# Moving three small VectorE operations ahead of two additions, and turning round the first score products of one visit in six

## The chip, the cores and the metric

The kernel runs on one core of a Trainium2 chip. The metric is the device time of one execution in microseconds (us). The engines are named as in the profile: PE is TensorE's matmul side, PEld its weight loads, DVE is VectorE, ACT is ScalarE, POOL is GpSimd, SP is SyncE.

## The reference

The input is x, 32 images of 256 channels and 32 x 32 positions, all in float32. For each image:

```python
h = _gn(x)                                  # group norm: 32 groups of 8 channels
q, k, v = 1x1 convolutions of h             # 8 heads of 32 channels, 1024 tokens
scores = q k^T / sqrt(32), kept only where key < query
out = x + softmax(scores) v
```

The group norm takes the mean and the variance of each group of eight channels over all positions. The mask is strict: a token doesn't see itself, and the first token's attention is zero.

## The kernel before

**Staging.** The kernel works through the images in one long pipeline of visits. An image has two channel groups `g` of 128 channels (four heads each), and a group has six visits (`VISITS`, L557), so an image has `N` = 12 visits. A visit computes scores of some key blocks against some query ranges for all four heads, exponentiates them on ACT, and adds the results up for the softmax's denominators on DVE. Keys lie on the partitions, so the exponentials go straight into the second product as the moving operand.

**The loop around the change** is at L705. In iteration i it calls, in this order:

1. `scores(i)` (L339): products into three two-bank PSUM tiles `sT` (L302), then three exponentials on ACT, into `e` (L384) and `eh` (L380), and, where the visit touches the diagonal, two masks on POOL (`mask`, L330).
2. what is listed in `at` for i: projections of a coming image (`pp` and `ppv`, L162) and some steps of older images.
3. `values(i - 1)` (L399): products of the exponentials of the visit before with v, into `acc` (L409).
4. `add_keys(i - 1)` (L421): the additions on DVE (L427), one to three of them.
5. what is listed in `after` for i: preparation of a coming image, output of an older one (`finish`, L521: `num` and `rb` on DVE, then a store), sums of denominators through DMAs.

[...] `FINISH` (L627) puts outputs of the image two before at the visits 1, 2 and 4, and `finish` of one visit precedes the preparation of the next.

**Preparation of an image** is `prepare` (L611) with the offsets `PREPARE` (L624), counted in visits from the image's first. It has ten steps: statistics of the two channel groups (`norm_channels`, L172), `norm_mean` (L180: four small products of `mv` with the averaging matrix into `pm`, and its eviction on ACT to `mean`), `norm_deviation` (L188: three DVE operations on 128 x 2 elements, L195 to L197, which wait for `mean`), `norm_variance` (L200: the second statistics product `pv`, which waits for `dev`, and its eviction to `rstd`), `norm_rstd` (L211, on POOL), and four times `norm_apply` (L221, on ACT). `norm_mean` and `norm_deviation` both stand at offset -9, `norm_variance` at -8, all of them in `after`. PSUM tiles for `pm`, `pv`, and half of the projections come from one pool with a single buffer (`misc`, L124), so `pv` also waits until the projection before it has been copied out (`v`, L266). Image 0's preparation runs ahead of the loop, image 1's has a list of offsets of its own (L668), and images 2 to 31 use `PREPARE` (L678).

**Scores of a visit.** The heads 0 to 3 of a group take 32 rows of the array each, and the two halves of a 128-key block take 64 columns each, so there are eight tiles of 32 x 64. A float32 product is carried out in two passes, which have a record each in the trace. An entry of a visit's list is "long" (to the `sT` tiles of heads 0, 1 and of heads 2, 3) or "short" (to the third tile). A `pair` (L282) is a short entry made of two products for each half: one 128 columns wide and one 64 wide, on the diagonal. `scores_of` (L307) carries out an entry's products by their place n in the pair: all 128-column ones first, then, after a call of `between`, the 64-column ones. `scores` does first the shorts of heads 2 and 3, then the longs of heads 0 and 1 (from the last entry of the list to the first), then the first long of heads 2 and 3, and then, behind a semaphore, the shorts of heads 0 and 1, and what is left.

Visit 0 of each group has two longs, of 384 and of 128 columns, and a pair; it is at `PAIRS` (L566). Visit 5 has two longs of the same widths and a short of 256 columns, and is not in `PAIRS`. The other four have a single long of 512 columns.

## Time and profile before

| | |
|---|---|
| median of 3 runs | 1832.91 us (1831.83 to 1835.73) |
| the profiled execution's own time | 1833.38 us |
| its span, first to last instruction | 1831.7 us |
| granted TensorE clock | 0.998 |
| DVE, busy share of the span | 91% |
| ACT, busy share of the span | 79% |
| DMA queues, share of 16 engines | 36.4% (software), 27.1% (hardware) |
| time of a whole image in the middle of the run | 56.1 us |

The page gives the busy time of each engine, then the chain of work that ended last, then groups of instructions with what ended the idle time before them. A line of the timeline begins with the start in us from the span's start and the duration; `x16` is the number of records merged in it, and the bracket at its end is the idle time of the engine before it and who ended it. The records of matmuls are pipelined: their starts are measured and their ends are modelled, so that a record can start ahead of the end of the one before.

### The profile page before, as it was taken

Reading aid. Unit: us, or ns where it says so; the run is one execution under the profiler, and the core shown is the slowest. Engines: PE = TensorE matmul, PEld = TensorE weight load, DVE = VectorE, ACT = ScalarE, POOL = GpSimd, SP = SyncE. Lnnn points to the kernel's source line nnn. Section 1 sums busy time; section 2 is a strip of 40 time slices with the busy share of each in tenths; the row PEclk is TensorE's granted clock in tenths of the full one; section 3 lists DMA queues with packets and bytes.
Section 4 is the critical chain, followed back from the end, with each engine's and each line's share of the span. In section 5 each row is a group of like instructions: output and inputs, shape, how many; then the busy total and the mean of one; then the engine's idle time right before and its main releaser. Section 6 shows DMA issues by size and latency. Waiting matters only on the chain.

```text
span 1831.7 us, 81670 instructions
## 1 busy us (share of the span) xinstructions
PE 1798.4 (98%) x37036; PEld 961.7 (53%) x37036; DVE 1667.8 (91%) x1831; ACT 1454.9 (79%) x1985; POOL 780.6 (43%) x901
## 2 busy tenths in 40 slices
PE   9999999999999999999999999999999999999997
PEld 5555555555555555555555555555555555555553
DVE  4689999999999999999999999999999999899988
ACT  6888878888778888788887788877888878788784
POOL 2344444444443444444434444444444344343431
PEclk9999999999999999999999999999999999999999
DMA  3457676676766676666767666667667676666652
GB/s 122 72 97 145 129 141 118 133 150 128 141 124 134 135 144 128 139 122 133 148 129 146 117 133 145 132 133 137 128 130 143 129 140 119 133 144 132 124 112 84
DMA packets 86531, 236.77 MB, mean 129 GB/s; under 512 B 21281, under 2 KB 22305, under 8 KB 70305
## 3 DMA queue, kind: packets, MB, share of 16 engines
q0 software_dynamic: 15872, 97.53, 36.4%
q1 hardware_dynamic: 70304, 133.96, 27.1%
q8 instruction: 290, 4.75, 1.1%
q14 instruction: 65, 0.52, 0.1%
HBM read 66.85 MB, written 34.57 MB: 55 GB/s over the span
## 4 chain that ended last, share of the span: by engine, by line
PE 93%; DVE 6%; issue 1%; ACT 0%; POOL 0%; DVEq 0%; POOLq 0%
PE sT L302 30%; PE pp L162 26%; PE acc L409 25%; PE ppv L162 10%; DVE e L427 3%; DVE dev L196 1%; DVE dev L197 1%; PE pd L461 1%; PE pv L162 0%; PE busy L148 0%; DVE rb L533 0%; ACT e L384 0%; DVE diagonal L427 0%; DVE dev L195 0%; PE pm L162 0%
## 5 line engine op out<-in xcount | busy, mean ns | idle before, releaser
L384 ACT ACTIVATE e<-sT 128x1024 f32<-128x1024 f32 x768 | 744.5, 1022 | 256.5 <-PE sT L302 232.2
L330 POOL TENSOR_SCALAR_AFFINE_SELECT diagonal<-eh 128x512 f32<-128x512 f32 x512 | 515.2, 1028 | 892.0 <-ACT eh L380 892.0
L302 PE MATMUL sT<-q,k 32*64 32x128 f32 (+2 forms) x18432 | 584.8, 372 | 3.3 <-issue 3.1
L427 DVE TENSOR_TENSOR e<-e,e 128x1024 f32<-128x1024 f32 x314 | 549.7, 1751 | 25.7 <-ACT v L266 6.3
L302 PEld LDWEIGHTS sT<-q,k 32*64 32x64 f32 x18432 | 406.1, 131 | 183.4 <-PE sT L302 59.4
L162 PE MATMUL pp<-xn,wT 128*32 128x512 f32 x4096 | 494.2, 598 | 0.9 <-issue 0.7
L409 PE MATMUL acc<-e,v 128*32 128x512 f32 (+3 forms) x4608 | 403.5, 450 | 0.0
L380 ACT ACTIVATE eh<-sT 128x768 f32<-128x768 f32 (+1 forms) x384 | 341.7, 890 | 0.0
L409 PEld LDWEIGHTS acc<-e,v 128*32 128x32 f32 x4608 | 150.1, 110 | 260.8 <-issue 238.3
L162 PE MATMUL ppv<-wT,xn 128*32 128x256 f32 x4096 | 248.5, 382 | 0.0
L162 PEld LDWEIGHTS pp<-xn,wT 128*32 128x32 f32 x4096 | 107.5, 109 | 201.4 <-issue 166.4
L427 DVE TENSOR_TENSOR diagonal<-diagonal,e 128x1536 f32<-128x1536 f32 x126 | 188.3, 1495 | 17.0 <-PE acc L409 9.2
L427 DVE TENSOR_TENSOR e<-e,eh 128x1024 f32<-128x1024 f32 x126 | 181.5, 1441 | 6.8 <-ACT xn L235 0.5
L427 DVE TENSOR_TENSOR e<-e,diagonal 128x2048 f32<-128x2048 f32 x63 | 144.0, 2286 | 36.8 <-POOL diagonal L330 36.8
L409 PEld LDWEIGHTS acc<-diagonal,v 128*32 128x32 f32 x4096 | 123.1, 110 | 86.8 <-issue 75.3
L162 PEld LDWEIGHTS ppv<-wT,xn 128*32 128x32 f32 x4096 | 120.9, 109 | 79.9 <-issue 7.8
L409 PE MATMUL acc<-diagonal,v 128*32 128x128 f32 x4096 | 161.2, 273 | 0.0
L440 POOL DMA_DIRECT2D diagonal<-diagonal x124 | 111.5, 899 | 64.3 <-DMA diagonal<-diagonal 64.3
L235 ACT ACTIVATE xn<-x,shift,rstd 128x256 f32<-128x256 f32 x248 | 137.1, 613 | 0.0
L528 DVE SCALAR_TENSOR_TENSOR rb<-num,v_bias_col,x 128x256 f32<-128x256 f32 x248 | 117.7, 515 | 4.4
L440 POOL DMA_DIRECT2D e<-e x124 | 102.2, 824 | 38.2 <-issue 38.2
L526 DVE TENSOR_TENSOR num<-num,rb 128x512 f32<-128x512 f32 x124 | 110.7, 893 | 0.5 <-DMA rb<-inverses 0.5
(78 smaller groups left out, 1026.1 us busy)
## 6 DMA issues: line engine op xcount, KB each, us to landing
diagonal<-diagonal POOLq DMA_DIRECT2D x62, 512.0 KB, 6.4
e<-e POOLq DMA_DIRECT2D x62, 512.0 KB, 5.6
rb<-inverses SPq DMA_DIRECT2D x124, 256.0 KB, 4.6
out_dram<-rb SPq DMA_DIRECT2D x124, 256.0 KB, 5.2
x<-in_x_dram SPq DMA_DIRECT2D x120, 256.0 KB, 5.8
diagonal<-diagonal POOLq DMA_DIRECT2D x62, 256.0 KB, 4.9
folded<-diagonal SPq DMA_DIRECT2D x62, 256.0 KB, 3.3
e<-e POOLq DMA_DIRECT2D x62, 256.0 KB, 5.1
```

The source lines that it names most:

```text
L162: nc.tensor.matmul(out[part], lhsT=lhsT[:, part], rhs=rhs, start=start, stop=stop, skip_group_check=True)
L196: nc.vector.tensor_mul(dev, dev, dev)
L235: nc.scalar.activation(to, of, AF.Identity, bias=live["shift", b][:, g : g + 1], scale=rstd)
L302: return nc.tensor.matmul(bank[c : c + KEYS, cols], lhsT=live["k", b, g][rows, kb * P + c : kb * P + c + KEYS], rhs=live["q", b, g][rows, ...
L330: nc.gpsimd.affine_select(out=square[:, :, place + s * P : place + (s + 1) * P], in_=raw[:, :, (1 - s) * KEYS : (3 - s) * KEYS], pattern=[ ...
L380: exp = nc.scalar.activation(eh.rearrange("p (n bank) q -> p bank n q", n=2)[:, :, :, :narrow], short[:, :, :, :narrow], AF.Exp)
L384: nc.scalar.activation(e[:, 2 * a : 2 * a + 2, :wide], pairs[a][:, :, :wide], AF.Exp)
L409: nc.tensor.matmul(acc[HD * j : HD * (j + 1), of], lhsT=live["v", b][:, kb, h * HD : (h + 1) * HD], rhs=e[:, j, :], start=first, stop=last ...
L427: nc.vector.tensor_add(to, to, tile_of(b, g, at))
L440: nc.gpsimd.dma_start(out=total[:rows], in_=total[rows : 2 * rows], accum_op=ALU.add)
L526: nc.vector.tensor_mul(num, num, rb)
L528: nc.vector.scalar_tensor_tensor(blocks(rb, s), blocks(num, s, s == 1), v_bias_col[:, g : g + 1], blocks(xt[:, g, cols], s), ALU.add, ALU.add,
```

## The change

Two things are changed.

- A third list, `between`, is carried out between `values` and `add_keys` of an iteration. For the images 2 to 31, `prepare` puts `norm_mean` and `norm_deviation` there (the steps with k = 2 and 3), in the same iteration as before.
- `scores_of` takes an order for the places n. In visits that have two longs and a pair, which is visit 0 of each group, the shorts of heads 2 and 3 begin with the 64-column products; the 128-column long of heads 0 and 1 follows as their `between`, then come the 128-column products of the pair, and then the 384-column longs. The shorts of heads 0 and 1 keep their order.

```diff
-        def scores_of(b, g, bank_of, heads, entries, between=lambda: None):
+        def scores_of(b, g, bank_of, heads, entries, between=lambda: None, order=slice(None)):
...
-                for n in range(max(map(len, halves))):
-                    if n:
+                for k, n in enumerate(list(range(max(map(len, halves))))[order]):
+                    if k:
                         between()
...
-            first = short_of((2, 3))
-            for n in range(len(longs) - 1, -1, -1):
-                long_of((0, 1), n)
+            begin = [lambda n=n: long_of((0, 1), n) for n in range(len(longs) - 1, -1, -1)]
+            if i in PAIRS and len(longs) > 1:
+                first = short_of((2, 3), begin.pop(0), slice(None, None, -1))
+            else:
+                first = short_of((2, 3))
+            for f in begin:
+                f()
             long_of((2, 3), 0)
...
-        at, after = {}, {}
+        at, between, after = {}, {}, {}
...
                 if n is None:
                     f()
+                elif isinstance(n, tuple):
+                    when(n[0], f, between)
                 else:
                     when(n, f, after)
...
-                    prepare(b, [first + n for n in PREPARE])
+                    prepare(b, [(first + n,) if k in (2, 3) else first + n for k, n in enumerate(PREPARE)])
...
                     values(b, v)
+                    for f in between.pop(i, ()):
+                        f()
                     if b < B - 1 or v not in SUMMED or v == 1:
                         add_keys(b, v)
```

More of the change, by code (lines that the diff above doesn't have):

```diff
@@ L348, in scores @@
             short = pairs[2].rearrange("p bank (n q) -> p bank n q", n=2)
-            short_of = lambda heads, *between: scores_of(
-                b, g, lambda j: short[:, j % 2, j // 2, :], heads, shorts, *between
+            short_of = lambda heads, *how: scores_of(
+                b, g, lambda j: short[:, j % 2, j // 2, :], heads, shorts, *how
             )
@@ L722, in unshifted @@
                     f()
-            assert not at and not after
+            assert not at and not between and not after
             outside = end_last(B - 1)
```

## The prediction

> **What bounds the kernel now.** I read the page's first part, then the list of waits, then the timeline at the two places that the diff touches. First the busy time of the engines:

> ```profile
> PE 1798.4 (98%) x37036; PEld 961.7 (53%) x37036; DVE 1667.8 (91%) x1831; ACT 1454.9 (79%) x1985; POOL 780.6 (43%) x901
> ```

> TensorE (PE) stands for 33 us of a span of 1831.7. It sets the end; a microsecond that it stops waiting for, or does in less, is a microsecond of the result, as long as VectorE (DVE, 91%) keeps up. In the list of waits (engine, line waited at, who ended it: us in total, times, longest) two lines concern the second statistics product, `pv`:

> ```profile
> PEld pv L162 <- ACT v L266: 18.0, 20, 0.9
> PE pv L162 <- DVE dev L197: 16.4, 27, 1.1
> ```

> So half of PE's idle time lies ahead of `pv`. One of the 27 (0.39 us, at 32.6 us) is image 1's, which the change leaves as it is: 16.0 us over 26 remain. Here is one, in the timeline of all engines (start, duration, engine, line, operation):

> ```profile
> 709.50 0.17 ACT L185 ACTIVATE mean<-pm 128x2 f32<-128x2 f32 x1 [0.86 <-PE pm L162]
> ...
> 710.84 0.14 DVE L533 COPY rb<-x 128x1 f32<-128x1 f32 x1
> 710.90 1.21 DVE L427 TENSOR_TENSOR e<-e,e 128x1024 f32<-128x1024 f32 x1
> 712.04 1.22 DVE L427 TENSOR_TENSOR e<-e,eh 128x1024 f32<-128x1024 f32 x1
> ...
> 713.05 0.61 ACT L266 COPY v<-ppv 128x512 f32<-128x512 f32 x1
> 713.17 0.15 DVE L195 TENSOR_TENSOR dev<-mv,mean 128x2 f32<-128x2 f32 x1
> ...
> 713.35 0.62 PE L409 MATMUL acc<-diagonal,v 128*32 128x128 f32 x16
> ...
> 713.36 0.54 DVE L196 TENSOR_TENSOR dev<-dev 128x2 f32<-128x2 f32 x1
> 713.93 0.55 DVE L197 TENSOR_TENSOR dev<-dev,mv 128x2 f32<-128x2 f32 x1
> ...
> 714.63 0.24 PE L162 MATMUL pv<-dev,avg 128*32 128x2 f32 x8 [0.66 <-DVE dev L197]
> ...
> 714.80 1.55 PE L302 MATMUL sT<-q,k 32*64 32x256 f32 x48
> ```

> The mean is there at 709.67. DVE is then still at an older image's output (`rb`, to 710.98), does the two additions of the visit, and only then the three small operations of the deviation, which end at 714.48; PE had nothing to do from 713.97. In a few images PE came late for other reasons and found `dev` ready; TensorE's own timeline shows one:

> ```profile
> 1332.44 0.62 PE L409 MATMUL acc<-diagonal,v 128*32 128x128 f32 x16
> 1332.88 0.22 PE L162 MATMUL pv<-dev,avg 128*32 128x2 f32 x8
> 1333.03 0.64 PE L302 MATMUL sT<-q,k 32*64 32x256 f32 x13
> ```

> From the last values to the next scores it takes 0.59 us here (1332.44 to 1333.03) and 1.45 in the other (713.35 to 714.80). The wait therefore costs 0.86, 0.20 more than the idle time says, since unhindered matmuls start ahead of the modelled end of those before.

> The other place is a visit whose scores have two long pieces and a pair (64 of the 384 visits), here beside the visit after it:

> ```profile
> 719.43 1.57 PE L302 MATMUL sT<-q,k 32*64 32x128 f32 x64
> 720.93 1.92 PE L162 MATMUL pp<-xn,wT 128*32 128x512 f32 x16
> ...
> 724.08 1.47 PE L302 MATMUL sT<-q,k 32*64 32x128 f32 x48
> 725.48 1.92 PE L162 MATMUL pp<-xn,wT 128*32 128x512 f32 x16
> ```

> Both put 704 columns through each of the eight tiles of the array, but the first takes 1.50 us to the next product (719.43 to 720.93) and the second 1.40 (medians of all: 1.496 and 1.404).

> [...] `dev` started 3.5 us after its mean was there. [...] in the visit at 719.43 the 128-column products of heads 0 and 1, written after the 64-column ones of heads 2 and 3, start at 0.053 us and those at 0.269. The measurement decides: I treat the two pairs of heads as two queues. [...] a mask of POOL takes 0.63 us alone and 2.07 at 741.75 beside an addition.

> **The change, step by step.** The order of instructions moves at 30 places on DVE and at 64 on PE; ACT, POOL and SP keep theirs, and no DMA is passed.

> *Deviation.* `norm_mean`'s four products and its eviction stay where they were on PE and ACT. On DVE the three operations come ahead of the visit's two additions. DVE is free for them at 710.98, the mean is there at 709.67, so DVE waits for nothing new (margin 1.31 us; image 2, which has no outputs to finish there, would wait, once, for under 2 us, with 2.2 us of DVE idle time close by). The three take 0.47 us where POOL is quiet (0.15, 0.16, 0.16 in image 2) and 1.29 in the timeline above, where POOL masks. They end by 711.5 to 712.3; `pv` wants them, with 0.15 us from DVE's end to PE's start (714.48 to 714.63), at 713.8: covered by at least 1.3 us. The next term is the copy `v` on ACT, whose PSUM buffer `pv` takes: it ends at 713.66, and with the same 0.15 it lets `pv` start at 713.81 where unhindered PE would start at 713.79. So the wait goes down to at most 0.02. Gain: 16.0 + 26 x 0.20 = 21.2 us. Delayed by the move: the two additions, by 0.5 to 1.3 us. They release buffers that are used again at 717.8 (`eh`, three buffers, two visits on) at the earliest, 3 us later: no cost.

> *Scores.* Single records of the visit at 719.43, from its first start, in ns, first and second pass: heads 2 and 3: 128 columns 0 and 160, 64 columns 269 and 325, then the first of four 384-column products at 383 but the other three at 462 to 496. Heads 0 and 1: 128 columns at 53 and 213, 384 columns at 322 and 645. In the visit at 724.08 the four products after the 64-column ones all start at 383 to 403. The difference: at 322 and 325 both queues start a product[...], eight weight loads (131 ns each) compete, and heads 2 and 3 need theirs 58 ns later. In the new order, from the steps seen (a cold first pass takes its columns at 0.83 ns and 54 ns more; otherwise 109 for 128 columns, 56 for 64): heads 2 and 3: 64 columns 0 and 107, 128 columns 163 and 272, 384 columns 381 and 704. Heads 0 and 1 begin at 27, as in visit 5 of a group, where also eight records stand ahead of them (four products of two passes, not eight), and reach their 384 at 296. The loads for 381 can begin at 272, 109 ns ahead instead of 58, and not together with those of 296. I take it that the ragged start goes and the visit falls to the 1.404 of its neighbour: 0.092 us. Bounds: 0.12 (the earlier start of heads 0 and 1 counts too), nothing, and below nothing another collision of the same size, 0.09 lost. Gain: 64 x 0.092 = 5.9 us, from -6 to 7.7. The new first product waits for ACT as the old one did.

> *Does DVE keep up?* DVE stands twice in an image's 56.1 us:

> ```profile
> 744.44 2.29 DVE L427 TENSOR_TENSOR e<-e,diagonal 128x2048 f32<-128x2048 f32 x1 [1.11 <-POOL diagonal L330]
> ...
> 755.77 0.99 DVE L427 TENSOR_TENSOR e<-e 128x512 f32<-128x512 f32 x1 [0.63 <-PE acc L409]
> ```

> The second is true slack: DVE waits for PE's values. The first is not wholly: POOL's mask at 741.75 is held up by DVE's own addition (741.03 to 743.32), and DVE then waits for the mask. PE would want an image in 56.1 - 0.86 - 2 x 0.09 = 55.1 us; DVE as it stands needs 56.1 - 0.63 = 55.5. So DVE falls behind by some 0.4 us an image, until the mask gets in ahead of the addition and the 1.11 shrinks. It takes less than a microsecond of lag for that, and `dev` bears 1.3. I expect this balance, at no cost.

> *Sum.* The profiled execution took 1833.38 us (span 1831.7 and 1.7 around it), the median shown is 1832.91, 0.5 less, within their spread of 3.9. 1833.4 - 21.2 - 5.9 = 1806.3 us.

> **Rivals.**
> - *DVE becomes the bound.* If the mask's wait stays 1.11, the image takes DVE's 55.5 us: 0.63 x 29 = 18.3 us saved, 1815.1. For it: 91% busy, slack of 0.63. Against: the mask follows PE and ACT, DVE lags, so they part.
> - *The order of the scores gives nothing*, because the two queues collide elsewhere: 1833.4 - 21.2 = 1812.2.
> - *Slower: additions stuck behind the wait for the mean.* DVE takes the deviation in order, so where it arrives before the mean, the additions and all after them stand. DVE has 0.63 of slack and PE can't run ahead of it for long, so a stand of w makes the image 55.5 + w: slower by over 0.2% from w = 0.76 on. DVE would have to come 2.1 us earlier than 710.98. At w = 1.0 it gives 0.37 x 29 = 10.7 us more, 1844. Against it: the 2.3 us of outputs in front of it in every image from the third on.

> **Chances.** Forecast 0.70 (by itself 1802 to 1810), DVE bound 0.12, scores give nothing 0.13, slower 0.05. The range from 1802 to 1815 takes in the bounds of the scores and nearly all of the first two rivals, and leaves out the slow one. A measurement can tell 0.2% (3.7 us) from no change: faster 0.94, within 0.01, slower 0.05.

> **What would show it.** The waits lose "PE pv <- DVE dev", last values to scores becomes 0.59 to 0.65 in every image, `dev` stands ahead of the additions with no wait for `mean`; visits with two long pieces and a pair fall from 1.50 to about 1.40; DVE's 0.63 vanishes and its 1.11 shrinks. Wrong if `pv` still waits for `dev` (DVE lags too far) or for `v`, or if a new wait of DVE for `mean` stands near 711.

## The result and the profile after

The changed kernel took 1814.57 us (median; 1810.73 to 1815.51), beside 1832.37 for the kernel before on the same chip (1831.3 to 1835.73): a ratio of 0.9896, 95% interval 0.9876 to 0.9915. It is faster, inside the range of the prediction and 8.3 us above its forecast of 1806.3. The profiled execution took 1814.37 us, its span is 1812.7. Line numbers of the changed kernel are 4 higher than those of the kernel before from L380 on. First the page's busy times:

```profile
PE 1795.4 (99%) x37036; PEld 954.8 (53%) x37036; DVE 1674.0 (92%) x1831; ACT 1457.5 (80%) x1985; POOL 867.2 (48%) x901
```

TensorE now stands for 17 us of the span (33 before). The list of waits no longer has a line of 27 for `pv` behind `dev`. What is left on these operations is one wait of image 1, and one of `dev` for its mean:

```profile
DVE e L431 <- PE acc L413: 32.2, 29, 12.1
...
DVE e L431 <- POOL diagonal L330: 21.6, 32, 1.1
...
ACT rstd L209 <- PE pv L162: 15.1, 30, 0.8
...
DVE dev L195 <- ACT mean L185: 2.1, 1, 2.1
...
PE pv L162 <- DVE dev L197: 0.4, 1, 0.4
```

ACT's wait for `pv` was 35.9. DVE's two waits in the first two lines were, before:

```profile
DVE e L427 <- PE acc L409: 44.1, 34, 12.2
DVE e L427 <- POOL diagonal L330: 36.8, 33, 1.1
```

The timeline of all engines at the same preparation as the one shown of before (start, duration, engine, line, operation):

```profile
703.06 0.14 DVE L537 COPY rb<-x 128x1 f32<-128x1 f32 x1
703.12 0.14 DVE L195 TENSOR_TENSOR dev<-mv,mean 128x2 f32<-128x2 f32 x1
...
703.30 0.16 DVE L196 TENSOR_TENSOR dev<-dev 128x2 f32<-128x2 f32 x1
703.50 0.16 DVE L197 TENSOR_TENSOR dev<-dev,mv 128x2 f32<-128x2 f32 x1
703.67 1.23 DVE L431 TENSOR_TENSOR e<-e,e 128x1024 f32<-128x1024 f32 x1
...
705.57 0.62 PE L413 MATMUL acc<-diagonal,v 128*32 128x128 f32 x16
...
706.01 0.22 PE L162 MATMUL pv<-dev,avg 128*32 128x2 f32 x8
...
706.16 1.31 PE L302 MATMUL sT<-q,k 32*64 32x256 f32 x32
```

`dev` is done at 703.66, 2.3 us before `pv`, and takes 0.54 us, not 1.31: POOL's masks start only after it, at 705.48. From the last values to the scores it is 0.59 us (705.57 to 706.16). In 28 of the images 2 to 31 it is 0.58 to 0.62; in the other two it is 0.69 and 0.76, and no wait for `dev` stands there either. Before, it was over 0.65 in 26 of these images, 1.46 in most.

Visit 0 of the second channel group takes 1.419 to 1.420 us in all 32 images (1.496 before). Visit 0 of the first group does so in images 0 to 3 only. After that 24 of 28 take longer, up to 2.24, in sum 8.9 us. Here is one (TensorE's matmuls and weight loads, image 8):

```profile
461.12 1.46 PE L302 MATMUL sT<-q,k 32*64 32x64 f32 x59
...
462.98 0.33 PE L302 MATMUL sT<-q,k 32*64 32x64 f32 x5 [0.40 <-issue]
462.98 0.19 PEld L302 LDWEIGHTS sT<-q,k 32*64 32x64 f32 x4 [0.54 <-issue]
```

After 59 of 64 records both sides of TensorE stop and then go on together. No semaphore ends that idle time: "issue" is the profile's word for time in which an engine waited for nothing that the profile shows. This stall is new, and it is about as large as what is missing.

**What the stalls have in common.** The record before which PE stops is number 63 of the visit (counted from 0) in image 4, 62 in image 5, 61 in image 6, and so on, one earlier in each image: a place fixed in the instruction stream, not in the work. Counted over all records of TensorE in the order of their starts (matmuls, weight loads and a few others; 74,151 here), these places lie at 193 modulo 256. And the list of DMA queues has two of the kind "instruction"; the larger, q8, moved this much:

```profile
q0 software_dynamic: 15872, 97.53, 35.7%
q1 hardware_dynamic: 70304, 133.96, 28.0%
q8 instruction: 290, 4.75, 1.1%
```

That gives two theories for the missing 8 us. *Late blocks:* the transfers of the kernel have moved against TensorE, and the packet that brings the block for visit 0 of the first group starts later (mostly 0.9 to 1.6 us ahead of the visit, about 1.8 before). *Order:* the new order of the scores itself stumbles in that visit. The expectations of the first runs below call them F (fetch) and O.

### The profile page after: what moved, and what is told of

Same layout as the page of the kernel before. It is cut to its first block, busy times and chain, and to the rows that moved or that the text cites. A ratio compares the mean times of both kernels' runs of the same rounds, so it can differ in the third digit from the quotient of the medians.

```text
span 1812.7 us, 81670 instructions
## 1 busy us (share of the span) xinstructions
PE 1795.4 (99%) x37036; PEld 954.8 (53%) x37036; DVE 1674.0 (92%) x1831; ACT 1457.5 (80%) x1985; POOL 867.2 (48%) x901
## 4 chain that ended last, share of the span: by engine, by line
PE 98%; DVE 1%; issue 0%; ACT 0%; DMA 0%; POOL 0%
PE sT L302 31%; PE acc L413 27%; PE pp L162 26%; PE ppv L162 13%; PE pd L465 1%; DMA x<-in_x_dram 0%; ACT e L388 0%; DVE st L177 0%; PE pv L162 0%; PE pm L162 0%; DVE rb_last L532 0%; ACT eh L384 0%; DVE rb_last L520 0%; DVE turned L517 0%; DVE acc L530 0%
## 5 line engine op out<-in xcount | busy, mean ns | idle before, releaser
L330 POOL TENSOR_SCALAR_AFFINE_SELECT diagonal<-eh 128x512 f32<-128x512 f32 x512 | 618.6, 1230 | 840.8 <-ACT eh L384 839.5
L431 DVE TENSOR_TENSOR e<-e,e 128x1024 f32<-128x1024 f32 x314 | 571.0, 1818 | 25.7 <-ACT v L266 4.2
L302 PE MATMUL sT<-q,k 32*64 32x128 f32 (+2 forms) x18432 | 587.5, 372 | 3.2 <-issue 2.5
L302 PEld LDWEIGHTS sT<-q,k 32*64 32x64 f32 x18432 | 397.1, 131 | 197.2 <-PE sT L302 69.6
L162 PE MATMUL pp<-xn,wT 128*32 128x512 f32 x4096 | 495.0, 598 | 1.1 <-issue 0.8
L162 PE MATMUL ppv<-wT,xn 128*32 128x256 f32 x4096 | 247.8, 382 | 0.0
L162 PEld LDWEIGHTS pp<-xn,wT 128*32 128x32 f32 x4096 | 107.7, 109 | 199.7 <-issue 167.9
L431 DVE TENSOR_TENSOR diagonal<-diagonal,e 128x1536 f32<-128x1536 f32 x126 | 194.9, 1547 | 16.9 <-PE acc L413 9.2
L431 DVE TENSOR_TENSOR e<-e,eh 128x1024 f32<-128x1024 f32 x126 | 166.0, 1317 | 6.8 <-DVE e L431 0.5
L162 PEld LDWEIGHTS ppv<-wT,xn 128*32 128x32 f32 x4096 | 121.4, 109 | 78.7 <-issue 7.0
L530 DVE TENSOR_TENSOR num<-num,rb 128x512 f32<-128x512 f32 x124 | 123.3, 994 | 0.6 <-DMA rb<-inverses 0.6
```

Source lines behind the costliest of these rows:

```text
L162: nc.tensor.matmul(out[part], lhsT=lhsT[:, part], rhs=rhs, start=start, stop=stop, skip_group_check=True)
L302: return nc.tensor.matmul(bank[c : c + KEYS, cols], lhsT=live["k", b, g][rows, kb * P + c : kb * P + c + KEYS], rhs=live["q", b, g][rows, ...
L330: nc.gpsimd.affine_select(out=square[:, :, place + s * P : place + (s + 1) * P], in_=raw[:, :, (1 - s) * KEYS : (3 - s) * KEYS], pattern=[ ...
L431: nc.vector.tensor_add(to, to, tile_of(b, g, at))
L530: nc.vector.tensor_mul(num, num, rb)
```

## The experiments

Each was timed beside the kernel before on the same chip. In the lines of code, `-` and `+` mark what the run takes out and puts in.

**Each half alone.** The deviation alone:

```diff
-            if i in PAIRS and len(longs) > 1:
+            if False:
```

> Only the deviation is moved; the scores keep their old order. Theory F (fetch): what is missing of the forecast are stalls of PE for its own instructions near the end of the first group's visit 0; they come because DVE lags PE once pv no longer waits, so that POOL's mask and with it the 512 KB fold of denominators start later against PE and hold up the 16 KB fetch of PE's next instructions. Then they are here too: first group's visit 0 at a mean of 1.70 to 1.80 us instead of 1.50, second group's at 1.50, time 1818 to 1822. Rival O (order): the stalls belong to the new order of the score products, which makes the visit denser. Then both groups stay at 1.50 and the time is 1810 to 1812.

Measured: 1819.39, ratio 0.9920 (0.9906 to 0.9934). Visit 0 of the first group takes longer than its 1.496 in 15 images, up to 2.27, in sum 4.7 us; in the second group all 32 take 1.496 to 1.498. The stalls are there with the old order of the scores: *order* falls. The scores alone:

```diff
-                    prepare(b, [(first + n,) if k in (2, 3) else first + n for k, n in enumerate(PREPARE)])
+                    prepare(b, [first + n for n in PREPARE])
```

> Only the order of the score products is changed; the deviation stays behind the additions, so pv waits as before. F: no stalls; visit 0 takes 1.42 us in both groups, time 64 x 0.077 = 4.9 us below before, 1827 to 1828. O: first group's visit 0 at a mean of about 1.69 as in the changed kernel, second at 1.42: 6 us lost, 2.5 gained, 1835 to 1837.

Measured: 1829.28, ratio 0.9971 (0.9961 to 0.9982), by the ratio 5.3 us (3.3 to 7.1). Visit 0 takes 1.419 in both groups with three exceptions, and the waits of `pv` are those of before (18.0 and 16.3). So the scores' half is worth what its visits show, and the stalls come with the deviation's half, which moves DVE.

**Where the blocks end.** The direct test of late blocks: the changed kernel with instructions that do nothing of use, ahead of the first image, so that all later blocks end elsewhere in the work.

```diff
+            pt = ps_s.tile([P, 2, HALF], F32, tag="sT", name="phase")
+            for _ in range(5):
+                product(pt[:, 0, :2], ident, ident[:, :2])
```

> The changed kernel with five small products of two columns (40 products and loads of each kind, 80 PE instructions, under 1 us) behind the warm-up, which moves every 16 KB boundary of PE's instruction stream 80 instructions ahead in the program. F: the stalls leave records 63 to 36 of the first group's visit 0, since its boundary lies some 40 products earlier; time changes with where the boundaries now fall against the DMAs, between 1804 and 1820. B and O: visit 0 keeps its stalls at the same records, time within 1 us of the changed kernel's.

Measured: 1807.41 (1805.3 to 1808.66), ratio 0.9851 (0.9836 to 0.9866): 80 instructions more and 7 us less. The visit of image 8, by TensorE's own timeline, without a stop:

```profile
462.44 1.49 PE L302 MATMUL sT<-q,k 32*64 32x64 f32 x64
463.86 1.93 PE L162 MATMUL pp<-xn,wT 128*32 128x512 f32 x16
```

All 32 take 1.42 us. In visit 0 of the second group four images now take longer (up to 2.48); the three larger stalls stand again at record 193 of 256. The kernel before with the same 80 instructions:

> The kernel before with the same five small products behind the warm-up (80 PE instructions more). If the boundaries of PE's instruction blocks cost the kernel before as little as its profile says (some 4 us of idle time outside pv, much of it taken back at pv's wait), F expects 1830 to 1836: the shift helps only where DVE lags. If the 80 instructions are worth 7 us in any kernel (rival P), 1825 to 1828.

Measured: 1831.38, ratio 0.9993 (0.9985 to 1.0001). The 80 instructions are no gain in themselves. Then the deviation alone with them (the edits of the first and the third experiment together), and 160 and 32 instructions instead of 80 (`range(10)`, `range(2)`):

> The changed kernel with the deviation's move alone (visit 0 in its old order), and 80 more instructions of TensorE ahead of the first image, which shift where its blocks of 256 instructions end. If the deviation is worth the forecast 21.2 us and only the late blocks took part of it: 0.988 of the kernel before (1812 of 1833), with visit 0 of the first group at 1.50 us in nearly every image. If the late blocks have no part in it and the step is worth only what it gave without the shift: 0.992 again (1819).

Measured: 1812.54, ratio 0.9894 (0.9879 to 0.9909), with visit 0 of the first group at 1.50 in all 32 images: as late blocks expected. Late blocks stand elsewhere, though, so the hit on 1812 is partly luck (the count by images below).

> The changed kernel with 160 more instructions of TensorE ahead of the first image instead of 80. The theory of late blocks: the time depends on where the blocks end; none of them can then end in visit 0 of the first group at the place where the changed kernel has its stalls, so that visit stays at 1.42 us; stalls elsewhere stand again at the same record of a block, 193 of 256, and the time lies between 1806 and 1815. If the 80 instructions helped by something else than the blocks' ends (a later start of TensorE, say): 1807 again or less, and no record in common to what stalls are left.

Measured: 1800.25 (1800.19 to 1801.94), ratio 0.9827 (0.9814 to 0.9841). This is the best version: faster than both kernels. Visit 0 of the first group is at 1.42 throughout, as late blocks expected, and only 9 blocks come within 1.65 us of their packet. But the time is 6 us below the bottom of the expectation: I had taken 1806 for the time without stalls, and it isn't. By the time alone the run would even fit the other branch (1807 or less). Four images stop in visit 0 of the second group; their stops lie at or near the block's end, between records 186 and 210, with one at 193. The count by images below tells the branches apart. The busy times of this run:

```profile
PE 1786.2 (99%) x37116; PEld 950.0 (53%) x37116; DVE 1673.2 (93%) x1831; ACT 1455.8 (81%) x1985; POOL 876.1 (49%) x901
```

> The changed kernel with 32 more instructions of TensorE ahead of the first image. The theory of late blocks: the ends of the blocks move 16 records ahead within visit 0 of the first group, whose stalls begin at record 47 and not 63 and go down by one an image; the transfer that brings the block starts some 0.4 us earlier against TensorE, so that the stalls become shorter or fewer: 1808 to 1814. If the place has nothing to do with it: the stalls stay where they are, 1814.6.

Measured: 1817.72, ratio 0.9919 (0.9905 to 0.9932). The place was hit exactly: the stalls begin at record 47 in image 4 and go on at 46, 45, 44, 43, 40, 39. They sum to 3.5 us in this visit (8.9 before the shift). The time missed: it is 3 us longer, not shorter, since other blocks' ends now fall into visit 4 and the projections of visit 5, where stops of up to 2.0 us stand in images 8 to 16. One visit's stalls don't tell the sum of all.

> The kernel before with 160 more instructions of TensorE ahead of the first image: what the shift alone does for it, so that the changed kernel's 1800.3 with the same shift can be compared with its own counterpart. If the two edits themselves are worth 21 + 5 us wherever the blocks end: 1825 to 1828. If the shift does nothing here and the 1800.3 are the change's own (32 us): 1832. If the shift takes away all stalls of the kernel before as well (some 14 us): 1818, and the edits would be worth 18.

Measured: 1842.7, ratio 1.0056 (1.0042 to 1.0069). All three expectations missed. The shift which made the changed kernel faster makes the kernel before slower by 10 us. Visit 0 of its second group stalls in images 2 to 11 (6.5 us in sum), and its list of waits shows what else grew:

```profile
PEld pv L162 <- ACT v L266: 25.4, 28, 0.9
PE pv L162 <- DVE dev L197: 20.1, 30, 1.1
```

They were 18.0 and 16.4. Both lines are of the same product, its weight load and its matmul, so they are not added up: TensorE's own wait is 3.7 us longer. In the old order a moved block end also changes how often `pv` is waited for; the new order has no such wait to lengthen.

**What delays the packet.** POOL issues the sums over partitions (`fold`) as DMAs of 512 KB, and the third of each image starts near visit 0 of the first group (`SUMS`: visits 3, 7, 10, 13). It starts 2.66 us ahead of that visit before and 2.03 after, since it follows DVE, which lags. Two visits later (the two steps that follow this fold move with it, in this run and the next):

```diff
-        SUMS = (3, 7, 10, 13)
+        SUMS = (3, 7, 12, 13)
```

> The changed kernel with the third fold of an image (the 512 KB DMA on POOL that runs while the first group's visit 0 begins) issued two visits later, behind that visit's masks; nothing left out. F: first group's visit 0 falls to 1.42 in nearly all images, unless the moved fold meets another fetch; time 1805 to 1808. Rival B (DVE is the bound and the stalls only fill the time that PE has in hand): the stalls go but waits come elsewhere, time 1813 to 1816.

Measured: 1856.67, ratio 1.0133 (1.0108 to 1.0157): a miss. Visit 0 of the first group is at 1.42 but for 7 images, and now blocks come late in the visits 1, 2 and 4 (means over both groups 1.51, 1.51 and 1.55, against 1.41, 1.48 and 1.46). In all, 64 blocks come within 1.65 us of their packet (47 in the changed kernel). One visit earlier, `SUMS = (3, 7, 9, 13)`:

> The changed kernel with the third fold one visit earlier, ahead of the mask of visit 10; nothing left out. F: it no longer runs when the block for visit 0 is fetched, so visit 0 of the first group falls to 1.42; the mask comes 0.8 us later, which DVE may have to wait for: 1805 to 1812. B: no gain, 1814 to 1820.

Measured: 1832.46, ratio 0.9993 (0.9979 to 1.0006): a miss again. Visit 0 of the first group stalls in 29 images, 28.7 us in sum. TensorE's timeline shows one with 2.09 us:

```profile
523.58 0.85 PE L302 MATMUL sT<-q,k 32*64 32x384 f32 x26
526.51 0.34 PE L302 MATMUL sT<-q,k 32*64 32x64 f32 x6 [2.09 <-issue]
```

The kernel before with its third fold held up by five small POOL operations ahead of it:

```diff
+            if (n, rows) == (2, 2 * HD):
+                for _ in range(5):
+                    nc.gpsimd.memset(inv_last, 0.0)
```

> The kernel before with five small memsets of a spare tile on POOL (some 0.6 us in all) ahead of an image's third fold, nothing else: DVE, ACT and PE keep their order. F: the fold and with it PE's fetch come as late against PE as in the changed kernel, so stalls appear at records 63 to 36 of the first group's visit 0, which goes from 1.50 to a mean of 1.60 to 1.85 us, while the second group's stays; time 3 to 11 us above before. Rival D (the stalls come with DVE's lag by itself, not by the fold): visit 0 stays at 1.50, time within 2 us of before.

Measured: 1830.63, ratio 0.9988 (0.9980 to 0.9996): a miss. The fold starts 1.30 us ahead of the visit, later than in the changed kernel, but the packet still starts 1.85 us ahead and comes in time. So a late fold alone isn't the cause. Last, the changed kernel with less for DVE: it leaves out one addition of each channel group (64 in all), so that the denominators lack those keys.

```diff
-            [(("L", 2, Q(0, 2)), ("L", 1, Q(2, 4))), (("L", 2, Q(2, 4)), ("H", 2, Q(0, 2)))],
+            [(("L", 2, Q(0, 2)), ("L", 1, Q(2, 4)))],
```

> The changed kernel without the second of the two additions that stand behind the deviation (62 or 64 additions of 128 x 1024 left out, 1.2 to 1.6 us of DVE an image twice; the denominators lack these keys). F: DVE no longer lags, its wait for the mask grows back to about 1.1 us, the fold starts 2.6 us ahead of visit 0 again, and visit 0 falls to 1.42 in nearly every image: 1804 to 1808. Rival O2 (a faster PE outruns its fetch whatever DVE does): stalls stay, 1812 to 1816.

Measured: 1814.43, ratio 0.9905 (0.9891 to 0.9920). Half a miss: the fold starts 4.0 us ahead, the packet mostly 1.8 to 2.7, and visit 0 of the first group is back at 1.42 in all but two images; but the time stays, with other blocks late (visit 4's mean 1.50 instead of 1.46).

**All of them together.** For each run, the stalls at the starts of blocks can be summed: the time from one PE record to the next at such a place, less the median of the same pair of records over the images, where that is over 0.15 us (images 3 to 29).

| kernel | late blocks, us | time, us | 1800.3 + 1.3 x (late - 1.4) |
|---|---|---|---|
| changed, 160 more | 1.4 | 1800.25 | |
| changed, 80 more | 4.9 | 1807.41 | 1804.9 |
| changed | 10.9 | 1814.57 | 1812.7 |
| changed, an addition less | 11.5 | 1814.43 | 1813.4 |
| changed, 32 more | 13.9 | 1817.72 | 1816.6 |
| changed, fold early | 26.5 | 1832.46 | 1832.9 |
| changed, fold late | 44.9 | 1856.67 | 1856.9 |
| before | 7.3 | 1832.37 | |
| before, 80 more | 3.9 | 1831.38 | |
| before, 160 more | 9.4 | 1842.7 | |

The factor 1.3 is fitted through the first and the last of the changed kernels (56.4 us over 43.5); the five between come within 2.5 us of it. The first, second, third and fifth differ only in where blocks end. The kernel before doesn't follow the line. (The late blocks are those of one profiled execution each, the times are medians.)

Counted by whole images, nothing needs to be fitted. An image runs from the start of its visit 0 to that of the next; here is image 9 in the kernel before (56.12 us), then in the changed kernel with 160 instructions more (55.09):

```profile
522.55 1.57 PE L302 MATMUL sT<-q,k 32*64 32x128 f32 x64
...
578.67 1.57 PE L302 MATMUL sT<-q,k 32*64 32x128 f32 x64
```

```profile
516.13 1.49 PE L302 MATMUL sT<-q,k 32*64 32x64 f32 x64
...
571.22 1.49 PE L302 MATMUL sT<-q,k 32*64 32x64 f32 x64
```

Call a block late when its packet ended less than 1.65 us before TensorE began it. The second column is the median of the images without a late block; all columns are of the profiled execution's images 2 to 30.

| kernel | without a late block, us | images with one | time over it, sum, us | profiled time less that, us |
|---|---|---|---|---|
| before | 56.115 | 14 | 4.6 | 1828.8 |
| before, 80 more | 56.115 | 25 | 1.9 | 1829.4 |
| before, 160 more | 56.12 | 14 | 13.6 | 1829.1 |
| before, fold delayed | 56.115 | 12 | 2.2 | 1829.1 |
| scores alone | 55.961 | 14 | 3.1 | 1823.9 |
| deviation alone | 55.246 | 23 | 13.1 | 1804.3 |
| deviation alone, 80 more | 55.246 | 17 | 9.3 | 1803.6 |
| changed | 55.091 | 26 | 15.0 | 1799.3 |
| changed, 32 more | 55.092 | 24 | 18.8 | 1799.0 |
| changed, 80 more | 55.091 | 21 | 9.5 | 1798.8 |
| changed, 160 more | 55.091 | 8 | 2.3 | 1799.4 |
| changed, an addition less | 55.089 | 18 | 15.9 | 1798.5 |
| changed, fold late | 55.092 | 25 | 53.9 | 1799.7 |
| changed, fold early | (55.67) | 26 | 34.5 | 1798.5 |

Images without a late block agree to 0.03 us in every run, with four exceptions: the only three of the early fold are 0.40 to 0.68 us above 55.09 (from which its sum is counted), with packets that ended 1.65 to 1.76 us ahead, and one of the kernel before with 160 more is 0.41 longer for another reason. Some images with a late block are shorter than the column says in the kernel before with 80 more (down to 55.65, for the wait of `pv` had shrunk there), and are taken off its sum. With the time over it taken off, the changed kernel is at 1798.5 to 1799.7 us in all seven runs, the one with 64 additions less for VectorE among them. This is why I call late blocks shown as the cause of the changed kernel's shortfall.

The traces show one thing more: before, the wait for `pv` hid late blocks. In image 21 of the kernel before, TensorE stalls for 0.37 us at a block's start in visit 4, just ahead of `pv`; the image still takes 56.12 us, and from the values to the scores it is 0.96 us, not 1.46. With the fold delayed, image 11 stalls for 0.94 us in that visit, at 56.12 us all the same. In the kernel before with 160 more, all stalls of over 0.15 us at a block's start but one lie in visits 6 and 7, behind the `pv` of that stretch, and its images do get longer.

## Why the prediction was right, and what it missed

- **Deviation: right in its mechanism, put too low in sum.** The wait is gone in all 26 images that had it, there is no wait for `v` beyond it, and the one wait for `mean` (2.1 us, image 2) was foretold, as under 2. An image without a late block gets 0.87 us shorter by this step (56.115 to 55.246), where the prediction read 0.86 from one place. In sum it is worth more than forecast: 0.87 over 29 images is 25.2 us, against 21.2, which counted only the waits that stood in the trace; where a late block had held TensorE up, they were shorter or none. By the times with 80 more on both sides it is 18.1 us (0.9894 against 0.9993, each with 0.08 to 0.15% to either side), for 9.3 us of late time are still in the one and 1.9 in the other.
- **Scores: right in what it does, mis-sized.** The term 0.092 us per visit measured 0.077 (1.496 to 1.419): not every ragged start went, since the second passes of the 384-column products still start between 708 and 764 ns, where the working had them all at 704. 64 x 0.077 is 4.9 us instead of 5.9; alone the edit gave 5.3 by the ratio. In the visit at 719.43 of before, one of the four weight loads for the 384-column products of heads 2 and 3 starts at 719.762, the other three at 719.893, 719.910 and 719.926, after four for heads 0 and 1 that start at 719.759 to 719.779 and take 0.132 us each. That such a collision made the start ragged is my estimate, from two visits; no run tests it.
- **"Does DVE keep up?" was right on the balance; its last words, "I expect this balance, at no cost", failed.** The balance came as put: DVE lags, and both of its waits shrink. VectorE's timeline, at the two places shown of before:

```profile
736.34 2.29 DVE L431 TENSOR_TENSOR e<-e,diagonal 128x2048 f32<-128x2048 f32 x1 [0.53 <-POOL diagonal L330]
...
747.16 0.99 DVE L431 TENSOR_TENSOR e<-e 128x512 f32<-128x512 f32 x1 [0.22 <-PE acc L413]
```

 In this image 1.11 became 0.53, and 0.63 became 0.22. But the step was not free. With the deviation moved, more blocks come late (47 instead of 23), and no wait for `pv` hides them any more: the time over the image without late blocks went from 4.6 to 15.0 us. It comes with the deviation's half (13.1 alone, 3.1 for the scores alone). That it is DVE's lag that makes blocks late is not shown: with an addition less the fold was early again, and 15.9 us of it stayed. No step of the prediction looked at the queue of instructions.
- **The sum.** The image without late blocks went from 56.115 to 55.091 us; the prediction had 56.1 and 55.1. Over 29 images that is 29.7 us, 2.6 more than the forecast of 27.1. The time over it grew by 10.4, which the forecast had at nothing. 29.7 - 10.4 is 19.3 us, and the profiled executions differ by 19.0. So the miss of 8.1 us (1806.3 to the profiled 1814.4) is a loss of 10.4 that was put at nothing, less 2.6 of gain that was left out; that the result still lies in the range owes something to luck.
- **The rivals that gave nearly this time are wrong all the same.** DVE as the bound was put at 1815.1. But the mask's wait did shrink, the same work of DVE runs in 1800.25 with 160 instructions more, and less work for DVE leaves the image at 55.09. Its price also left out that `dev` itself gets cheaper by 0.77 us an image (1.31 to 0.54) where POOL is quiet. Scores that give nothing, put at 1812.2: they gave 5. The slow rival had its wait for `mean` once, not in every image.
- **Luck of the place.** At three places of the blocks' ends the pair of edits is worth 17.8 us (1832.4 to 1814.6), 24.0 (1831.4 to 1807.4) and 42.5 (1842.7 to 1800.3). The forecast of 27.1 lies among them, and with 160 more the time would have been below the range. The kernel as it was measured has one of the poorer places.

What stays open is which transfers delay a packet, and how: the trace doesn't tell the engine of a packet. Moving the third fold and the two steps behind it changed the late blocks from 10.9 to 44.9 and 26.5 us, so they have a part; that a later fold did nothing to the kernel before shows that it isn't all.

## What to carry to other kernels

When an engine with tens of thousands of instructions is the bound, look for idle time that ends in "issue" and drifts by a fixed number of records from one repetition to the next. Here I read it as TensorE's wait for its own instructions: it stood at or near one record of 256 (193) whatever the work there was, and moving the blocks' ends by 80 instructions cleared the visit. A repeated wait that is taken away may have hidden other delays; here some of the late blocks had cost nothing as long as `pv` was waited for. Before a change of 1% is kept or dropped, measure it with the blocks shifted by two or three small amounts, since here the place alone moved one kernel between 1800 and 1818 us and the other between 1831 and 1843. Find the repetition that nothing disturbs and compare it with the forecast first: here it agreed to 0.03 us an image, and all of the rest was in the disturbed ones.

## What the runs showed of the hardware

- The packets of q8, 16 KB each and one for every 256 records of TensorE, took 0.88 to 1.96 us in the changed kernel (median 1.07), and in no run did PE begin a block less than 1.19 us after the end of the packet that I count to it. The packet for the next block started in the median 1.4 us after PE began the present one. By that reading there was one block of reserve, 6.3 us of work here (an estimate: 1812.7 over 289).
- VectorE carried out `dev` and the additions in the written order at the places shown. In image 2 of the changed kernel `dev` stood for 2.12 us until its mean was there, and the addition written behind it started at 93.50, when `dev` was done (93.48).
- A float32 product of the scores had two matmul records: visit 0 has 32 products and 64 records.
- Three VectorE operations of 128 x 2 elements took 0.14 to 0.16 us each at 703 us, where no mask of POOL ran beside them, and two of them 0.54 and 0.55 beside one.
- POOL's masks took 0.97 us in the median before and 1.08 after, the longest 2.41 and 2.71. They ran beside VectorE's additions more often: of 512, 162 overlapped none before (median 0.63 us) and 84 after (0.63), while 197 and 287 overlapped them for over three quarters of their time (medians 1.51 and 1.21). POOL's busy time rose by 87 us (780.6 to 867.2) with not one instruction more; an image without a late block still kept to the forecast.
